# An LSTM and a three-layer FFN on one core: loads of the beginning asked for in another order, and the last half of the outputs cut in two

## The chip, the core and the metric

One Trainium2 chip; the kernel runs on one of its cores. The metric is device time in microseconds (us): the median of three runs. Besides, one execution was taken by the profiler; its rows are times from the start of its span.

The engines are named as in the profile: PE is the matrix engine, PEld its weight loads, DVE the vector engine, ACT the scalar engine, POOL the GpSimd engine, SP the engine that only issues transfers. SPq, ACTq and POOLq are the queues in which SP, ACT and POOL issue transfers (DMAs).

## The reference

Cut to what matters (x is 32 x 64 x 256 in float32, cond is 32 x 256; every k is a matrix of booleans):

```python
xW = einsum('ntd,dg->ntg', x, Wx) + b              # g: 4 gates of 256
for t in range(64):                                # LSTM, h starts as cond, c as 0
    a = xW[:, t] + h @ Wh
    i, f, o = sigmoid(a[:, :256]), sigmoid(a[:, 256:512]), sigmoid(a[:, 512:768])
    g = tanh(a[:, 768:])
    c = f * c + i * g
    h = o * tanh(c)
y = concatenate([hs, -hs], -1)                     # FFN, weights +1 or -1
y = relu(s0 * (y @ sign(k0))) * 2                  # 512 -> 1024
y = relu(s1 * (y @ sign(k1))) * 2                  # 1024 -> 1024
out = x + s2 * (y @ sign(k2))                      # 1024 -> 256
```

## The kernel before, in words

**Layout.** 128 partitions hold 4 quarters of the hidden width times 32 sequences. The LSTM's products (line 246 for x times Wx, line 305 for h times Wh) are float32 and use the PE as four blocks of 32 columns at once; the trace shows each of these matmuls as two records. The FFN's products are float32r: every activation is split into a rounded part (h) and a rest (l), and both are multiplied by the same weights, one after the other, with the weights loaded again for each.

**Order.** The order of the work is written out by hand (a manual schedule); each engine carries out its instructions in the order of the program, and waits at an instruction until its inputs are there. The loop over the 64 steps (line 702) runs on PE the matmuls of a step's gates, and between them fillers: first products of x with Wx for later steps, from step 21 on the FFN of blocks of 16 steps (512 columns: 16 steps times 32 sequences). The last block (lines 417 to 583) comes after the last step, when no step is left to be mixed with.

**The beginning** (lines 107 to 156 and 637 to 682). DVE writes zeros: a small tile `warm`, then `idle` of 128 x 512 bf16, then the two rows for the bias. SP and ACT issue loads: the first eight steps of x (line 133: four transfers of 64 KB, two on each queue), Wx for the first 128 of the 256 inputs (k = 0) and then for the others (k = 1): two gates at once on SP (256 KB), the other two one by one on ACT (128 KB each). Then follow the next eight steps of x, and Wh. POOL issues the load of `h_first` and then those of the bias rows and scales. On PE, two matmuls of zeros clear the banks of the gates (line 641) and eight more go to a bank that is not read (`p_idle`, line 643, `WARM_UP = 8`). After them come the products of x: for eight steps the two middle gates with k = 0, then the two outer gates with k = 0, then the bias (line 658), then all four gates with k = 1. These need x turned round by DVE (line 229, two instructions of four steps each, behind all four loads of x) and the part of Wx concerned.

**Transfers and semaphores.** Transfers of SP and ACT share eight semaphores in turn; a transfer whose semaphore is still in use waits at its place in its queue until the one eight places earlier has landed.

**The end** (lines 550 to 583). The last layer of the last block has 128 output rows for m = 0 and as many for m = 1. The first eight of the 16 steps (half 0) are computed for both m, turned (line 385), scaled and added to x (line 388) and stored (line 380: four transfers of 64 KB, two on SP and two on ACT). The last eight steps (half 1) are computed for m = 0 and then for m = 1, each by 16 matmuls of 256 columns (8 blocks of inputs, h and l); each m is turned and scaled by itself, and one store of four transfers follows.

```python
        for m in range(2):
            layer2(1, m, [*range(K2, FC0), *range(K2)], True, True)
            turn_out(os[1], po_half[1, m], m)
            scale_out(os[1][:, :, m, :], xq[b, 1][:, :, ts(m, 32)])
        store(b, 1, os[1].rearrange("p t m j -> p t (m j)"), [nc.sync, nc.scalar])
```

## Time and profile before

| | |
|---|---|
| time, median of 3 runs | 312.36 us (312.21 to 312.55) |
| the profiled execution, whole time | 312.31 us |
| the profiled execution, its span | 310.5 us |
| PE busy | 304.5 us, 98% of the span, 4138 instructions |
| PEld busy | 242.7 us, 78% |
| DVE, ACT, POOL busy | 178.1, 142.0, 6.6 us |
| first warm-up matmul begins | 1.24 us |
| first product of x begins | 5.44 us |
| gates of step 0 begin | 16.84 us in the chain of waits |
| last matmul begins | 305.66 us |
| last instruction of DVE begins | 306.46 us |

The whole time has about 1.8 us outside the span. A row of the timeline has its start, how long it lasts, engine, line, operation, output and inputs, and in brackets the idle time before it with what ended it. The ends of matmuls are modelled: the distance from one start to the next is the better measure of their rate. In the chain of waits, each piece has its start, its length, and the engine and tile that the end of the kernel hung on in that time.

### The profile page before, as it was taken

To read this page: it belongs to the slowest core of one execution; us is meant where nothing else is said; L and a number is where in the kernel's file an instruction comes from. 1 tells how busy PE (TensorE), PEld (TensorE's weight loads), DVE (VectorE), ACT (ScalarE), POOL (GpSimd) and SP (SyncE) were. 2 spreads that over 40 slices of the span, in tenths; PEclk is the share of its full clock that TensorE was granted. 3 is DMA by queue.
4 is the path that set the end of the run, shared out by engine and by line. 5 is a ranking of instruction groups with operands and counts; after the bars stand their busy time and mean duration, and the time that the engine had idled before them with its cause. 6 is when DMAs were issued, how large, how long until landed. Compare 5 with 4: busy or idle time off the path is not lost.

```text
span 310.5 us, 9798 instructions
## 1 busy us (share of the span) xinstructions
PE 304.5 (98%) x4138; PEld 242.7 (78%) x4138; DVE 178.1 (57%) x530; ACT 142.0 (46%) x512; POOL 6.6 (2%) x24
## 2 busy tenths in 40 slices
PE   8999999999999999999999999999999999999994
PEld 4888888788777777777777777777777777899993
DVE  2566767777673444355754445567554434698543
ACT  0225566774564543435633434355443333886220
POOL 5300000000000000000000000000000000000000
PEclk9999999999999999999999999999999999999999
DMA  6874001142000000000010000000310000131002
GB/s 192 206 196 99 5 19 38 36 95 65 3 2 0 2 2 0 3 2 0 2 38 22 14 3 0 2 2 13 92 34 2 3 0 2 31 79 27 2 0 69
DMA packets 30587, 10.89 MB, mean 35 GB/s; under 512 B 27720, under 2 KB 29768, under 8 KB 30544
## 3 DMA queue, kind: packets, MB, share of 16 engines
q1 hardware_dynamic: 27136, 8.66, 11.2%
q10 hardware_dynamic: 3168, 1.57, 2.0%
q8 instruction: 32, 0.52, 0.7%
q0 software_dynamic: 240, 0.04, 0.1%
q14 instruction: 11, 0.09, 0.1%
HBM read 8.16 MB, written 2.10 MB: 33 GB/s over the span
## 4 chain that ended last, share of the span: by engine, by line
PE 97%; DVE 1%; ACT 0%; issue 0%; ACTq 0%
PE p L617 30%; PE gates L305 20%; PE px L246 18%; PE p L591 8%; PE po L604 7%; PE gates L452 4%; PE po L561 2%; PE r L452 2%; PE x L452 2%; PE p L479 2%; PE p_idle L643 1%; PE gates L641 0%; DVE a_7l L362 0%; DVE o L388 0%; PE p_bias L658 0%
## 5 line engine op out<-in xcount | busy, mean ns | idle before, releaser
L305 PEld LDWEIGHTS gates<-wh,hist 128*32 128x32 f32 x2016 | 54.6, 109 | 22.3 <-issue 13.4
L305 PE MATMUL gates<-wh,hist 128*32 128x192 f32 x2016 | 68.1, 275 | 0.0
L246 PE MATMUL px<-wx,xT 128*32 128x256 f32 (+1 forms) x1168 | 60.5, 353 | 0.1
L322 ACT ACTIVATE sig<-gates 128x128 f32<-128x128 f32 x64 | 17.7, 277 | 80.6 <-PE gates L305 80.4
L246 PEld LDWEIGHTS px<-wx,xT 128*32 128x32 f32 x1168 | 42.4, 110 | 11.3 <-DVE c_first L652 0.7
L326 DVE TENSOR_TENSOR kept<-sig,c 128x64 f32<-128x64 f32 x63 | 14.2, 225 | 50.0 <-ACT sig L322 49.7
L332 ACT ACTIVATE th<-c 128x64 f32<-128x64 f32 x64 | 16.4, 257 | 31.4 <-DVE c L330 31.4
L334 DVE TENSOR_TENSOR h<-sig,th 128x64 f32<-128x64 f32 x64 | 14.4, 225 | 20.7 <-ACT th L332 20.7
L262 DVE TENSOR_TENSOR xg<-px,bias 128x512 f32<-128x512 f32 x32 | 21.2, 671 | 2.8 <-PE px L246 2.3
L316 ACT COPY gates<-xg 128x192 f32<-128x192 f32 x64 | 20.0, 313 | 1.3 <-DVE xg L262 1.3
L591 PE MATMUL p<-hhi,w 128*128 128x512 f32 x48 | 19.3, 402 | 0.0
L591 PE MATMUL p<-hlo,w 128*128 128x512 f32 x48 | 19.1, 398 | 0.0
L339 DVE STREAM_TRANSPOSE hist<-h 128x64 f32<-128x64 f32 x64 | 15.7, 245 | 2.4
L330 DVE TENSOR_TENSOR c<-kept,new 128x64 f32<-128x64 f32 x64 | 14.4, 224 | 2.2
L324 ACT ACTIVATE sig<-gates 128x64 f32<-128x64 f32 x64 | 14.9, 233 | 0.1
L323 ACT ACTIVATE cand<-gates 128x64 f32<-128x64 f32 x64 | 14.0, 218 | 0.0
L328 DVE TENSOR_TENSOR new<-sig,cand 128x64 f32<-128x64 f32 x64 | 13.9, 217 | 0.0
L317 ACT COPY gates<-xg 128x64 f32<-128x64 f32 x64 | 13.0, 203 | 0.0
L591 PEld LDWEIGHTS p<-hhi,w 128*128 128x128 f32 x48 | 9.0, 188 | 2.2
L591 PEld LDWEIGHTS p<-hlo,w 128*128 128x128 f32 x48 | 9.0, 188 | 2.0
L211 ACT ACTIVATE w<-bits,nsgn,sgn 128x1024 fp32r<-128x1024 uint8 x8 | 9.9, 1241 | 0.0
L617 PE MATMUL p<-a_7h,w 128*128 128x512 f32 x24 | 9.9, 413 | 0.0
(249 smaller groups left out, 602.8 us busy)
## 6 DMA issues: line engine op xcount, KB each, us to landing
x<-in_x_dram SPq DMA_DIRECT2D x60, 64.0 KB, 2.8
out_dram<-o SPq DMA_DIRECT2D x28, 64.0 KB, 1.8
bits<-in_L_ffn_k_dram SPq DMA_DIRECT2D x10, 128.0 KB, 3.2
wx<-in_L_cond_Wx_dram SPq DMA_DIRECT2D x2, 256.0 KB, 4.2
wx<-in_L_cond_Wx_dram ACTq DMA_DIRECT2D x4, 128.0 KB, 4.6
wh<-in_L_cond_Wh_dram ACTq DMA_DIRECT2D x2, 256.0 KB, 5.6
wh<-in_L_cond_Wh_dram SPq DMA_DIRECT2D x2, 256.0 KB, 6.2
k<-in_L_ffn_k_dram SPq DMA_DIRECT2D x2, 256.0 KB, 3.1
```

What stands on the lines that cost most here:

```text
L246: nc.tensor.matmul(p[q * N : (q + 1) * N, t % 2, slots], xT[i // 2, i % 2][:, s, k, :], wx_q[:, k, q, slots], start=start, stop=False, ski ...
L262: nc.vector.tensor_tensor(xg[t], p.rearrange("p t g j -> p t (g j)"), b, ALU.add)
L305: nc.tensor.matmul(g[q * N : (q + 1) * N], hT[:, k, :], wh_q[:, k, q, slots], start=False, stop=(k == 1), skip_group_check=True,)
L316: nc.scalar.copy(gates[0], x_t[:, :3])
L322: nc.scalar.activation(sig[:, 0:2, :], gates[0][:, 1:3], AF.Sigmoid)
L324: nc.scalar.activation(sig[:, 2, :], gates[1][:, 0], AF.Sigmoid)
L332: nc.scalar.activation(th, c, AF.Tanh)
L339: nc.vector.transpose(hT, h.rearrange("p (j b) -> p b j", b=2))
L452: nc.tensor.matmul(bank[pair][:, i], a(k)[:, ts(2 * pair + i, P)], b(k, n), start=first and i == 0 and k == 0 and n == 0, stop=last and k ...
L591: nc.tensor.matmul(p, w0[:, k, ts(m, P)], a[:, k, :], start=(n == 0), stop=(n == 3))
L604: nc.tensor.matmul(po[m], w2[:, m, k], a1[k][n], start=(k == 0 and n == 0), stop=(k == FC1 - 1 and n == 1))
L617: nc.tensor.matmul(p1[m], w1[:, k, ts(m, P)], a0[k][n], start=(k == 0 and n == 0), stop=(k == FC0 - 1 and n == 1),)
```

## The change

At the beginning:

- `idle` becomes 128 x 128 and is written first; the matmuls of zeros read it four times over, so that they keep their 512 columns. `WARM_UP` goes from 8 to 7.
- The first eight steps of x are asked for in two halves of four steps (eight transfers of 32 KB). Between the halves, the two middle gates of Wx with k = 0 are asked for as two transfers of 64 partitions, one on each queue. After the second half come the outer gates with k = 0, one on each queue, then with k = 1 three gates at once on SP (384 KB) and the fourth on ACT.
- POOL issues the bias rows ahead of `h_first`.

At the end: half 1 with m = 1 is computed as two lots of four steps, each by 16 matmuls of 128 columns into a bank of its own; each lot is turned, scaled and stored by itself, with both m, as four transfers of 32 KB.

```diff
-    WARM_UP = 8
+    WARM_UP = 7
...
+    idle = const.tile([P, P], mybir.dt.bfloat16, name="idle")
+    nc.vector.memset(idle, 0.0)
     nc.vector.memset(warm, 0.0)
-    idle = const.tile([P, 512], mybir.dt.bfloat16, name="idle")
-    nc.vector.memset(idle, 0.0)
...
-    load_x(0, 0, both)
-    for k in range(2):
-        load_gates(wx, wx_d, (1, 2), [nc.sync], slice(k, k + 1))
-        for slot in (0, 3):
-            load_gates(wx, wx_d, (slot,), [nc.scalar], slice(k, k + 1))
+    first_x = [slice(0, SB // 4), slice(SB // 4, SB // 2)]
+    load_x(0, 0, both, first_x[0])
+    load_gates(wx, wx_d, (1, 2), both, slice(0, 1))
+    load_x(0, 0, both, first_x[1])
+    load_gates(wx, wx_d, (3,), [nc.sync], slice(0, 1))
+    load_gates(wx, wx_d, (0,), [nc.scalar], slice(0, 1))
+    load_gates(wx, wx_d, (1, 2, 3), [nc.sync], slice(1, 2))
+    load_gates(wx, wx_d, (0,), [nc.scalar], slice(1, 2))
...
-        for m in range(2):
-            layer2(1, m, [*range(K2, FC0), *range(K2)], True, True)
-            turn_out(os[1], po_half[1, m], m)
-            scale_out(os[1][:, :, m, :], xq[b, 1][:, :, ts(m, 32)])
-        store(b, 1, os[1].rearrange("p t m j -> p t (m j)"), [nc.sync, nc.scalar])
+        o = os[1].rearrange("p t m j -> p t (m j)")
+        ks = [*range(K2, FC0), *range(K2)]
+        layer2(po[1][:, :CB], 0, 1, ks, True, True)
+        turn_out(os[1], po[1][:, :CB], 0)
+        scale_out(os[1][:, :, 0, :], xq[b, 1][:, :, :32])
+        for i in range(2):
+            steps, p = ts(i, SB // 4), last_po[i][:, : CB // 2]
+            layer2(p, 1, 1, ks, True, True, ts(i, CB // 2))
+            turn_out(os[1][:, steps], p, 1)
+            scale_out(os[1][:, steps, 1, :], xq[b, 1][:, steps, 32:])
+            store(b, 1, o, [nc.sync, nc.scalar], slice(i * SB // 4, (i + 1) * SB // 4))
...
+    zeros = idle.unsqueeze(1).to_broadcast([P, TB // P, P])
     for g in gate_banks:
-        nc.tensor.matmul(g, idle[:, :P], idle, start=True, stop=True)
+        nc.tensor.matmul(g, idle, zeros, start=True, stop=True)
     for n in range(WARM_UP):
-        nc.tensor.matmul(p_idle, idle[:, :P], idle, start=True, stop=True)
+        nc.tensor.matmul(p_idle, idle, zeros, start=True, stop=True)
```

`store` gains an argument for the steps that it stores, and `layer2` takes the bank, the half and the columns in place of a table of banks. The matmuls of half 0 stay as they are, as does everything between the beginning and the end.

More of the change, by code (lines that the diff above doesn't have):

```diff
@@ L143, in lstm_ffn @@
     nc.scalar.activation(warm[:, 1:2], warm[:, :1], AF.Sigmoid)
-    h_first = const.tile([P, HQ], F32, name="h_first")
-    nc.gpsimd.dma_start(out=h_first, in_=cond.rearrange("n (q j) -> q n j", q=NQ))
     b_rows = b_d.rearrange("(o g h) -> o g h", o=1, g=4)
@@ L149, in lstm_ffn @@
     nc.gpsimd.dma_start(out=b_row[1][:1], in_=b_rows[:, 1:3])
+    h_first = const.tile([P, HQ], F32, name="h_first")
+    nc.gpsimd.dma_start(out=h_first, in_=cond.rearrange("n (q j) -> q n j", q=NQ))
     scales = []
@@ L375, in output, with store @@
             yield
-    def store(b, half, o, engines):
+    def store(b, half, o, engines, part=slice(0, SB // 2)):
         t0 = b * SB + half * (SB // 2)
@@ L380, in store @@
             engines[q % len(engines)].dma_start(
-                out=out[:, t0 : t0 + SB // 2, ts(q, HQ)], in_=o[q * N : (q + 1) * N]
+                out=out[:, t0 + part.start : t0 + part.stop, ts(q, HQ)], in_=o[q * N : (q + 1) * N, part]
             )
@@ L550, in last_block, with layer2 @@
         po = [ps_o.tile([P, TB], F32, tag="po", name=f"po{b}_{m}") for m in range(2)]
-        po_half = {
-            (0, 0): po[0][:, :CB],
-            (0, 1): po[0][:, CB:],
-            (1, 0): po[1][:, :CB],
-            (1, 1): ps_f.tile([P, TB], F32, tag="pf", name=f"po{b}_2")[:, :CB],
-        }
-        def layer2(half, m, ks, first, last):
+        last_po = [ps_f.tile([P, TB], F32, tag="pf", name=f"po{b}_{2 + i}") for i in range(2)]
+        def layer2(p, m, half, ks, first, last, cols=slice(0, CB)):
             for k in ks:
@@ L561, in layer2 @@
                     nc.tensor.matmul(
-                        po_half[half, m],
+                        p,
                         w2[:, m, k],
-                        a1[k, half][n],
-                        start=first and k == ks[0] and n == 0 and (half, m) != (0, 1),
+                        a1[k, half][n][:, cols],
+                        start=first and k == ks[0] and n == 0,
                         stop=last and k == ks[-1] and n == 1,
@@ L572, in last_block @@
             for m in range(2):
-                layer2(0, m, ks, ks[0] == 0, ks[0] > 0)
+                layer2(po[0][:, ts(m, CB)], m, 0, ks, ks[0] == 0 and m == 0, ks[0] > 0)
         for m in range(2):
-            turn_out(os[0], po_half[0, m], m)
+            turn_out(os[0], po[0][:, ts(m, CB)], m)
         o = os[0].rearrange("p t m j -> p t (m j)")
@@ L639, in lstm_ffn @@
     p_idle = ps_f.tile([P, TB], F32, tag="pf", name="p_idle")
+    zeros = idle.unsqueeze(1).to_broadcast([P, TB // P, P])
     for g in gate_banks:
-        nc.tensor.matmul(g, idle[:, :P], idle, start=True, stop=True)
+        nc.tensor.matmul(g, idle, zeros, start=True, stop=True)
     for n in range(WARM_UP):
-        nc.tensor.matmul(p_idle, idle[:, :P], idle, start=True, stop=True)
-    turn_x(0, 0, slice(0, SB // 4))
-    turn_x(0, 0, slice(SB // 4, SB // 2))
+        nc.tensor.matmul(p_idle, idle, zeros, start=True, stop=True)
+    for part in first_x:
+        turn_x(0, 0, part)
     for i in range(4):
```

## The prediction

> **What bounds the kernel now.** I read the page first, engines and then the chain that ended last:

> ```profile
> PE 304.5 (98%) x4138; PEld 242.7 (78%) x4138; DVE 178.1 (57%) x530; ACT 142.0 (46%) x512; POOL 6.6 (2%) x24
> ...
> PE 97%; DVE 1%; ACT 0%; issue 0%; ACTq 0%
> ```

> PE is busy in 98% of the span, and 97% of the chain that ended last lies on it. Between the first product of x and the last matmul no other engine stands in the chain for more than a few us, so the middle, which the change leaves alone, moves as one block. What counts is when PE starts useful work, whether it stalls early, and what follows its last matmul. So next comes the chain of waits for the first 12 us (start, length, what):

> ```profile
> 0.91 0.28 DVE idle L110
> 1.19 0.05 issue
> 1.24 1.03 PE gates L641 x2
> 2.27 3.23 PE p_idle L643 x8
> 5.51 1.89 PE px L246 x64
> 7.39 0.12 issue
> 7.51 1.96 PE px L246 x64
> ```

> PE waits for the zeros until 1.24, multiplies zeros until about 5.4, begins the products of x, and halts at 7.39: the second 64 records need the outer gates of Wx, which ACT asked for last. The timeline of the end:

> ```profile
> 305.54 0.28 PE L561 MATMUL po<-c_1h,w 128*128 128x256 f32 x1
> 305.54 0.19 PEld L561 LDWEIGHTS po<-c_1l,w 128*128 128x128 f32 x1
> 305.66 0.28 PE L561 MATMUL po<-c_1l,w 128*128 128x256 f32 x1
> 305.98 0.45 DVE L385 STREAM_TRANSPOSE o<-po 128x256 f32<-128x256 f32 x1 [0.95 <-PE po L561]
> 306.46 0.48 DVE L388 SCALAR_TENSOR_TENSOR o<-o,total,x 128x256 f32<-128x256 f32 x1
> 306.97 0.81 SPq L380 DMA_DIRECT2D out_dram<-o  x2
> 306.98 0.88 ACTq L380 DMA_DIRECT2D out_dram<-o  x2
> ```

> Matmuls of 256 columns start every 0.12 us. From DVE's start to the end of the span (310.5) pass 4.5 us: 1.0 on DVE, then the store.

> **The beginning, step by step.** (a) The zeros: DVE's 40-element fill took 92 ns and the 256-element one 272, so 0.83 ns an element; 64 elements take about 112 ns. Written first, from 0.82, they are there at 0.93, and PE starts 0.05 later at 0.98 instead of 1.24. (b) Nine matmuls of zeros instead of ten. Their weight loads start 0.427 us apart (2.07, 2.50, 2.92), while 512 columns later take 0.227 (line 479: 32 in 7.25): half the rate. The trace's record of the full clock starts at 5.20. Nine end at 0.98 + 9 x 0.427 = 4.82; about 0.10 lay between the last of them and the first product; so products start at 4.90 instead of 5.44. If the clock still comes at 5.20, the first 0.30 us run at half rate and lose 0.15: the gain is 0.54 - 0.15 = 0.39. If the clock comes 0.26 earlier with the work it is 0.5; if it comes half a us later, 0.1. I take 0.39, with the clock where the row has it. (c) The stall: one set of 64 records takes 1.75 us where nothing is missing (7.51 to the bias at 9.26). The first set should then be done at 5.44 + 1.75 = 7.19, and the second began at 7.51: 0.33 lost.

> Does the data come in time? Before, the 256 KB of x were followed by the middle gates (issued 1.66, landed at 5.0, three stragglers of 16 after 4.3, beside the 4 KB packets of `h_first`), and the outer ones landed at 6.15 and 7.38. After, only 128 KB of x stand ahead of the middle gates, whose halves go on both queues at about 1.6. First data came 1.0 us after an issue; 384 KB at the 200 to 270 GB/s of the transfer view are through by about 3.5, landed by 4 to 4.3, ahead of 4.90. The second half of x is needed at about 5.9; its second transfers wait for a semaphore of the first (about 2.7) and should land by 4.5. The outer gates, asked for at about 3.1, should land by 5.3 to 6.0; they are needed at 4.90 + 0.15 + 1.75 = 6.8. So the 0.33 goes; the bounds are nothing and all of it. Beginning: 0.39 + 0.33 = **0.72 gained**, bounds 0 and 0.9.

> At no cost: `h_first` is asked for some 2 us later and is first read by DVE at 14.04; it landed at 5.3. Queues: SP has 11 transfers ahead of the next x instead of 8, ACT 11 instead of 10. Wh is behind them; it landed at 14.9 and is needed at 16.84 before, at 16.1 after: 1.2 us of cover, which three more issues of 0.33 to 0.47 could just use up, but Wh's own wait is for earlier landings (issued only at 7.2 to 8.1), which come sooner.

> **The end, step by step.** (d) 16 matmuls of 256 columns become 32 of 128, and each still loads 128 x 128 weights. No row shows a float32r matmul under 256 columns. Columns alone: 512 take 0.227 and 256 take 0.120, so 128 would take 0.067. But weights must be in the array first, and where PE comes back from the gates, the weight loads show their own pace:

> ```profile
> 98.02 0.19 PEld L617 LDWEIGHTS p<-a_4l,w 128*128 128x128 f32 x1
> 98.13 0.19 PEld L617 LDWEIGHTS p<-a_5h,w 128*128 128x128 f32 x1
> 98.36 0.19 PEld L617 LDWEIGHTS p<-a_5l,w 128*128 128x128 f32 x1
> ```

> The first two are 0.11 apart, since the second starts once the first's matmul does, and nothing ran in front of it; the third waits for a matmul of 512 columns. 43 such pairs in the trace stand 108 or 109 ns apart, one 107, none closer. The load of 32 columns lasts 109 ns and that of 128 lasts 188: 0.82 ns a column, 105 for 128. So I take 0.109 a matmul: weights, not columns, set the pace. 32 x 0.109 - 16 x 0.120 = 3.49 - 1.92 = **1.57 lost**. Bounds: 0.067, 0.21 lost; 0.227, if 128 columns went at float32's four passes (line 305 does 512 columns of a step, all four blocks, in 0.87 where one pass of 512 is 0.21), 5.33 lost.

> [...]

> (e) The last matmul is shorter: 0.39 for 512 columns and 0.28 for 256 make 0.05 less for 128. (f) DVE's last two: turning took 0.245 for 64 columns and 0.45 for 256, so 0.31 for 128; scaling took 0.75 for 512 and 0.48 for 256, so 0.35. With their gaps 0.73 in place of 1.00: 0.27 gained. The lots are at least 16 x 0.067 = 1.07 apart, so the first lot's 0.73 on DVE is out of the way. (g) The last store moves 128 KB instead of 256. Before, 2.5 us passed from the first issue (306.97) to the last landing; the 256 KB moved in 1.3 of them (307.75 to 309.05), one queue's transfer behind the other's. Each queue's second issue still comes 0.36 to 0.42 after its first, and a store takes 1.8 to 2.0 to land. Half the data would save 0.65; with the issues in front, 0.40. Bounds 0 and 0.65. The first lot's four transfers are issued over a us earlier and are through by then; the semaphores that the last four wait for are those of half 0, landed long before.

> End: 1.57 - 0.05 - 0.27 - 0.40 = **0.85 lost**.

> **Sum.** 0.85 - 0.72 = 0.13 lost, on 312.31: 312.44. The profiled run is 0.05 under the median of 312.36, so I say 312.4. With i for the pace of the small matmuls the whole is 32 i - 3.36 us: nothing at i = 0.105, 0.62 lost at 0.124, 0.62 gained at 0.086. A measurement of this kernel can tell 0.2%, or 0.62 us, from no change.

> **Rivals.** *Columns set the pace* (i = 0.067): 1.22 gained, 311.1. For it: at 256 columns the pace is still the columns' (0.120 is 0.107 less than 512's). Against it: 44 pairs, none under 107 ns. It decides below i = 0.086. *Four passes* (i = 0.227): 3.9 lost, 316.2. It ends on the slow side, in the 32 small matmuls, and decides from i = 0.124. For it: no float32r row under 256 columns; against: 512 and 256 columns go at one pass. *The beginning gives nothing*: the middle gates land after 4.9, or the stall moves to another load, or Wh comes late. Then the end's 0.85 stands alone, 313.2. For it: landings had stragglers of up to 0.8 us; against: half as much is asked for ahead.

> **Numbers.** My forecast 0.60, columns 0.18, four passes 0.08, nothing at the beginning 0.14. The forecast's own range, with i from 0.105 to 0.120, the store's and the beginning's bounds, is 311.9 to 313.2; it is same in 0.44, slower in 0.10, faster in 0.06. The empty beginning is slower in 0.09, same in 0.05. Together: faster 0.06 + 0.18 = 0.24; same 0.49; slower 0.10 + 0.08 + 0.09 = 0.27. The range of 311.0 to 313.4 takes in the columns' case and the empty beginning and leaves out the four passes.

> **What would show it.** The first warm-up at 0.98, products at 4.9, no gap between the two sets of 64. Weight loads of the last 32 matmuls 0.109 apart: 0.067 or 0.227 decides for a rival. DVE's last two at 0.31 and 0.35, and 2.1 from the last first issue to the last landing. I am wrong if the chain has PE waiting for Wx or Wh, or if the middle gets longer.

## The result, and the profile after

| | before | after |
|---|---|---|
| time, median of four runs | 312.43 us (312.21 to 312.55) | 315.53 us (315.30 to 315.83) |
| ratio, 95% interval | | 1.0097, 1.0082 to 1.0112 |
| profiled execution, its span | 312.31, 310.5 us | 315.30, 313.3 us |
| first product of x | 5.44 us | 5.07 us |
| gates of step 0 on PE, in the chain | 16.84 us | 18.45 us |
| first matmul of the last quarter (half 1, m = 1) | 303.86 us | 305.49 us |

The change costs 3 us, and the prediction (312.4, at most 313.4) was wrong. One run of those below, of `e4_h_first` at 319.77 us, lies far above the others of its kernel and is left out of times and ratios as a slow one.

The page after, engines and chain:

```profile
PE 306.0 (98%) x4153; PEld 242.0 (77%) x4153; DVE 178.7 (57%) x532; ACT 142.1 (45%) x512; POOL 6.6 (2%) x24
...
PE 94%; DMA 3%; DVE 1%; ACTq 0%; ACT 0%; issue 0%
```

DMA, which had no share in the chain before, has 3% of it (9.6 us), and PE is down from 97 to 94%. The chain of waits of the first 20 us (start, length, what) says which transfers:

```profile
1.67 3.30 DMA wx<-in_L_cond_Wx_dram
4.97 0.02 issue
5.00 6.29 DMA wx<-in_L_cond_Wx_dram
11.29 0.04 issue
11.33 7.12 PE px L249 x128
18.45 0.87 PE gates L308 x32
```

Both pieces are Wx. The second is a transfer that is asked for only when the first has landed; it is one of the second rows (k = 1). PE's timeline shows what that did (in brackets the idle time before, and what ended it):

```profile
0.99 1.03 PE L647 MATMUL gates<-idle 128*128 128x512 bf16 x2 [0.99 <-DVE warm L110]
1.81 3.10 PE L649 MATMUL p_idle<-idle 128*128 128x512 bf16 x7
5.07 1.08 PE L249 MATMUL px<-wx,xT 128*32 128x128 f32 x32
6.56 2.83 PE L249 MATMUL px<-wx,xT 128*32 128x128 f32 x96 [0.41 <-DVE xT L232]
9.20 0.66 PE L664 MATMUL p_bias<-b_row,warm 128*32 128x128 f32 x16
11.33 7.12 PE L249 MATMUL px<-wx,xT 128*32 128x256 f32 x128 [1.48 <-DMA wx<-in_L_cond_Wx_dram]
```

PE starts 0.25 earlier as forecast, and its first product comes 0.37 earlier. Then it halts twice: 0.41 us for the second half of x, and 1.48 us for the second rows of Wx. The gates of step 0 come 1.61 us late, and from there the middle runs as one block: the last quarter starts 1.63 us late. The span is 2.73 longer, so the end has lost the other 1.10. Its timeline:

```profile
308.90 0.28 PE L560 MATMUL po<-c_1l,w 128*128 128x128 f32 x1
309.21 0.32 DVE L388 STREAM_TRANSPOSE o<-po 128x128 f32<-128x128 f32 x1 [1.08 <-PE po L560]
309.56 0.35 DVE L391 SCALAR_TENSOR_TENSOR o<-o,total,x 128x128 f32<-128x128 f32 x1
```

The 32 small matmuls start at 305.49 to 308.90, 0.110 us apart; DVE's two take 0.32 and 0.35; the last store is asked for at 309.94 and landed at 312.18, 2.24 us (before: 306.97 to 309.45, 2.48).

### The profile page after: what moved, and what is told of

It is laid out like the page before. It is cut to its first block, busy times and chain, and to the rows that moved or that the text cites. A ratio compares the mean times of both kernels' runs of the same rounds, so it can differ in the third digit from the quotient of the medians.

```text
span 313.3 us, 9842 instructions
## 1 busy us (share of the span) xinstructions
PE 306.0 (98%) x4153; PEld 242.0 (77%) x4153; DVE 178.7 (57%) x532; ACT 142.1 (45%) x512; POOL 6.6 (2%) x24
## 4 chain that ended last, share of the span: by engine, by line
PE 94%; DMA 3%; DVE 1%; ACTq 0%; ACT 0%; issue 0%
PE p L622 30%; PE gates L308 20%; PE px L249 17%; PE p L596 8%; PE po L609 7%; PE gates L455 4%; DMA wx<-in_L_cond_Wx_dram 3%; PE po L560 3%; PE r L455 2%; PE x L455 2%; PE p L482 2%; ACTq L93 0%; DVE a_7l L365 0%; DVE o L391 0%; DVE o L388 0%
## 5 line engine op out<-in xcount | busy, mean ns | idle before, releaser
L249 PEld LDWEIGHTS px<-wx,xT 128*32 128x32 f32 x1168 | 40.1, 110 | 15.8 <-DMA wx<-in_L_cond_Wx_dram 1.7
L327 ACT ACTIVATE sig<-gates 128x64 f32<-128x64 f32 x64 | 14.9, 232 | 0.2
```

The source lines that it names most:

```text
L249: nc.tensor.matmul(p[q * N : (q + 1) * N, t % 2, slots], xT[i // 2, i % 2][:, s, k, :], wx_q[:, k, q, slots], start=start, stop=False, ski ...
L327: nc.scalar.activation(sig[:, 2, :], gates[1][:, 0], AF.Sigmoid)
```

## Experiments

Ratios are to the kernel before on the same chip (312.6 to 312.8 us in these runs), with 95% intervals.

### The two parts by themselves

`e1_head_only`: all edits of the beginning, and lines 550 to 583 and `store` as before.

> The new beginning with the old end. In the changed kernel's trace the last layer's second half for m = 1 begins at 305.49 us, 1.63 later than before (303.86). Theory 'the beginning lost it, by late transfers of Wx': this kernel takes about 1.6 us more than before (314.0), gates of step 0 begin near 18.4 and PE halts about 1.5 us ahead of the k = 1 products. Rival 'the end lost it, the late start is an accident of one execution': 311.7, the 0.72 gained that was forecast.

Measured: 314.83 us, 1.0065 (1.0042 to 1.0088): 2.0 us lost. The first theory holds; in this profile PE waits 1.86 us for the second rows.

`e2_tail_only`: the reverse, the new end on the old beginning.

> The old beginning with the new end. Theory 'beginning and end add up': about 1.1 us more than before (313.5), the small matmuls 0.111 us apart, as in the changed kernel's trace. Forecast of the prediction: 0.85 more (313.3). Rival 'the columns set the pace': no loss or a gain of 0.45.

Measured: 313.77 us, 1.0040 (1.0027 to 1.0054): 1.25 us lost. The two make 3.3, the change 3.0: they add up, within the intervals. Both parts lose.

### The end, piece by piece

`e9_two_lots_alone`: only the matmuls are halved.

```diff
-            layer2(1, m, [*range(K2, FC0), *range(K2)], True, True)
+            lots = 2 if m else 1
+            for i in range(lots):
+                layer2(1, m, [*range(K2, FC0), *range(K2)], True, True, ts(i, CB // lots))
```

> The kernel before, with its beginning, its stores and its DVE work on the last half as they were; only the 16 last matmuls of 256 columns become 32 of 128 (both lots in one bank, turned and scaled together as before). This is step (d) by itself. By the pace of 0.111 us seen in the profile after: 32 x 0.111 - 16 x 0.120 = 1.63 lost, and nothing given back: 1.0052 times the kernel before. By the prediction's 0.109: 1.57, 1.0050. If instead the columns set the pace (0.067): 0.22, 1.0007.

Measured: 314.55 us, 1.0062 (1.0048 to 1.0077), 1.9 us lost (1.5 to 2.4). In its profile the 32 last matmuls take 3.41 us from the first start to the last, where the 16 took 1.80, and DVE and the store take what they took before (1.31 us to the first issue, 2.48 to the last landing). That is 1.61 us by the profile, as forecast, and within the interval of the times.

`e10_four_lots_alone`: the same with four lots (`lots = 4 if m else 1`), 64 matmuls of 64 columns.

> As the two lots alone, with 64 matmuls of 64 columns. If the weight load of 128 columns sets the pace of a small matmul, whatever its columns, they stand 0.108 to 0.111 apart: 64 x 0.111 - 1.92 = 5.2 lost, 1.0166 times the kernel before. If a part of the 0.111 was still the 128 columns' own time, half the columns go faster: at 0.08, 3.2 lost, 1.010.

Measured: 320.85 us, 1.0261 (1.0244 to 1.0279), 8.2 us lost instead of 5.2. Up to 308.06 the matmuls start 0.112 apart, as expected; from then on 0.2135. The table by stretches (length, then PE, PEld, DVE, ACT, POOL busy and their counts, then the granted clock, DMA share, GB/s):

```profile
306.00:308.00 2.00, 2.00 (x20) 2.00 (x19) 0.00 (x0) 0.00 (x0) 0.00 (x0) 1.00 0.25 55
308.00:310.00 2.00, 2.00 (x12) 2.00 (x11) 0.00 (x0) 0.00 (x0) 0.00 (x0) 0.51 0.00 0
310.00:312.00 2.00, 2.00 (x11) 2.00 (x11) 0.00 (x0) 0.00 (x0) 0.00 (x0) 0.50 0.00 0
```

The granted clock fell to 0.50 although PE was never without work. While the clock was whole, 64 columns (0.112) went no faster than 128 (0.110 after), so the columns did not set the pace here. That the load of 128 x 128 weights set it agrees with the prediction's 43 pairs of weight loads, 0.108 to 0.109 apart.

`e11_dve_by_steps_alone`: the 16 matmuls undivided; turning, scaling and stores of the last quarter by four steps.

```diff
-            turn_out(os[1], po_half[1, m], m)
-            scale_out(os[1][:, :, m, :], xq[b, 1][:, :, ts(m, 32)])
-        store(b, 1, os[1].rearrange("p t m j -> p t (m j)"), [nc.sync, nc.scalar])
+            for i in range(m + 1):
+                steps = slice(i * SB // 2 // (m + 1), (i + 1) * SB // 2 // (m + 1))
+                turn_out(os[1][:, steps], po_half[1, m][:, ts(i, CB // (m + 1))], m)
+                scale_out(os[1][:, steps, m, :], xq[b, 1][:, steps, ts(m, 32)])
+                if m:
+                    store(b, 1, os[1].rearrange("p t m j -> p t (m j)"), [nc.sync, nc.scalar], steps)
```

> The kernel before, with its 16 last matmuls of 256 columns, and only the turning, the scaling and the stores of the last quarter of the outputs by four steps at a time. With the matmuls undivided both lots come to DVE at once: four operations (0.32, 0.35, 0.32, 0.35, with gaps some 1.40) in place of two (0.97), and the last store is asked for 0.43 later, of half the size, which the profile after showed to land 0.24 sooner. So 0.1 to 0.3 lost, 1.0003 to 1.001, if the first lot's stores are through in time; up to 0.7, 1.002, if eight stores one behind the other take as long as four whole ones. If steps (f) and (g) of the prediction held by themselves (0.27 and 0.40 to the good), it would gain 0.2 here.

Measured: 313.38 us, 1.0024 (1.0014 to 1.0035), 0.75 us lost, the upper case of the forecast. By the profile DVE is done at 307.32, but the last store is asked for at 307.63: each queue is still busy with its second issue of the first lot. It landed 2.30 after that, against 2.48 for a whole one. So half a store saved about 0.2 here, and its issue, queued behind another, came 0.3 late.

### The beginning: three suspects of which two fall

`e3_k1_split`: the beginning of e1, with the second rows in the pieces of before.

```diff
-    load_gates(wx, wx_d, (1, 2, 3), [nc.sync], slice(1, 2))
+    load_gates(wx, wx_d, (1, 2), [nc.sync], slice(1, 2))
     load_gates(wx, wx_d, (0,), [nc.scalar], slice(1, 2))
+    load_gates(wx, wx_d, (3,), [nc.scalar], slice(1, 2))
```

> The new beginning with the old end, but Wx with k = 1 asked for as before: two gates at once on SP (256 KB), one and one on ACT (128 KB each), in place of 384 KB on SP and 128 KB on ACT. Theory 'the one transfer of 384 KB is what is late' (issued 4.54, landed 11.02): the stall ahead of the k = 1 products shrinks from 1.5 us to under 0.5, and about 1 us of the loss goes (313.0). Rival 'transfers are slow in that stretch whatever their size, or issued too late because of the eight semaphores': no change within 0.3 us of the new beginning alone.

Measured: 315.04 us, 1.0079 (1.0063 to 1.0095). That the second rows come as 384 KB in one transfer is not the cause.

`e4_h_first`: the beginning of e1, with `h_first` ahead of the bias rows, where it was.

> The new beginning with the old end, but h_first asked for ahead of the bias rows, as before. Theory 'its 4 KB packets, now at 5.4 to 6.9 us, hold up the engines just when Wx with k = 1 starts to move': that transfer lands 1 us sooner or more and the kernel gains about 1 us on the new beginning alone, if the middle gates do not land later for it. Rival 'the packets only share the engines': within 0.3 us of the new beginning alone.

Measured: 314.72 us, 1.0075 (1.0054 to 1.0096). By the times its place is not the cause either. In its profile, which is of the fastest run (313.79), the loss only sits elsewhere: the big transfer of the second rows landed at 10.52 in place of e1's 11.54, but the middle gates at 5.08 and 5.67 in place of 4.55 and 5.00, and PE began at 5.76.

`e5_x_whole`: the beginning of e1, with x's first eight steps in four transfers ahead of the gates.

```diff
-    load_x(0, 0, both, first_x[0])
+    load_x(0, 0, both)
     load_gates(wx, wx_d, (1, 2), both, slice(0, 1))
-    load_x(0, 0, both, first_x[1])
```

> The new beginning alone (the old end), but the first eight steps of x asked for whole, in four transfers of 64 KB ahead of the gates, in place of eight of 32 KB with the middle gates between them. Theory A: eight DMA semaphores go round, each transfer takes one, and the eight small transfers of x hold them, so that the second rows of Wx are asked for only at 4.54 us, when the middle gates have landed. Without the split the ninth transfer waits for a piece of x (landed at about 3.0), is asked for at about 3.1, and should land by 8.5 to 9.5, ahead of PE's need at 9.9: PE's wait of 1.5 to 1.9 us goes, and the time falls from 314.8 to 312.4 to 313.2. Theory B: not when the rows are asked for but the slow moving between 6 and 10 us (some 150 GB/s) makes them late, and it comes from what moves at that time, the broadcasts of the three scales above all: the rows still land at about 11, and the time stays at 314.4 to 315.2.

Measured: 313.15 us, 1.0022 (1.0008 to 1.0037): 1.3 of the 2.0 us come back, and the intervals of e1 and e5 do not touch. When SP asked for the big transfer of the second rows, before, after and in e5 (start, length):

```profile
2.15 0.43 SPq L127 DMA_DIRECT2D wx<-in_L_cond_Wx_dram  x1
4.54 0.35 SPq L127 DMA_DIRECT2D wx<-in_L_cond_Wx_dram  x1
2.97 0.35 SPq L127 DMA_DIRECT2D wx<-in_L_cond_Wx_dram  x1
```

The list of transfers has, of after (count, KB each, median us from issue to landing; x's are its first eight steps):

```profile
wx<-in_L_cond_Wx_dram SPq DMA_DIRECT2D x1, 384.0 KB, 6.5
x<-in_x_dram ACTq DMA_DIRECT2D x4, 32.0 KB, 2.7
```

and of e5:

```profile
wx<-in_L_cond_Wx_dram SPq DMA_DIRECT2D x1, 384.0 KB, 5.6
x<-in_x_dram ACTq DMA_DIRECT2D x2, 64.0 KB, 2.6
```

The big transfer itself is 0.9 us faster in e5; the greater part, 1.57 us, is when it is asked for. After, twelve transfers stand ahead of it, so the thirteenth waits for the semaphore of the fifth, half of the middle gates, which landed at 4.53: issue at 4.54, landing at 11.02. In e5 eight stand ahead, so it waits for a piece of x: issue at 2.97, landing at 8.54, well before PE's need at 10.0. In the kernel before, the transfer of the second rows was one of the first eight, waited for none, and was asked for at 2.15. e5 changes a second thing, for the whole of x now stands ahead of the middle gates: their second half landed at 5.67, and PE began at 5.76. That it is the semaphore which holds the second rows back is read from the rows, where in both profiles the issue follows that landing by 0.01 us.

On the size of a transfer the rows show: 32 KB took 2.6 us to land on SP and 2.7 on ACT, 64 KB in e5 2.4 and 2.6, so half the size landed no sooner. No run here tries the halves of the partitions by themselves. The price that counted here was another, a semaphore for each piece: the second rows were asked for at 4.54 in place of 2.97.

### What moves beside the second rows

`e6_scales_late`: the beginning of e1, with the three broadcasts of the scales on SP's queue behind the next block's x.

```diff
-        nc.gpsimd.dma_start(out=s, in_=s_d.partition_broadcast(P))
...
+    for s, s_d in zip(scales, (s0_d, s1_d, s2_d)):
+        nc.sync.dma_start(out=s, in_=s_d.partition_broadcast(P))
```

> The new beginning alone (the old end), but the three broadcasts of the scales (128 pieces of 4 bytes each) are taken off GpSimd's queue and asked for on SP's behind the loads of the next x. Theory A (the semaphores hold the second rows of Wx back): issue at 4.5 and a landing at about 11 remain, and the time stays at 314.4 to 315.2. Theory B (the broadcasts, moving from 6.7 to 12.4, slow everything beside them): the rows, still asked for at 4.5, land at 8.5 to 9.5, the stretch from 6 to 10 us moves over 220 GB/s in place of some 150, PE's wait at about 10 goes, and the time falls to 312.8 to 313.4.

Measured: 313.43 us, 1.0027 (1.0017 to 1.0037): 1.2 us come back, and the intervals of e1 and e6 do not touch. The same two stretches of e1 and then of e6 (last column GB/s):

```profile
6.00:8.00 2.00, 2.00 (x62) 1.98 (x57) 0.53 (x2) 0.00 (x0) 0.00 (x0) 1.00 0.66 163
8.00:10.00 2.00, 2.00 (x80) 1.90 (x71) 0.00 (x0) 0.00 (x0) 0.16 (x1) 1.00 0.58 126
```

```profile
6.00:8.00 2.00, 1.89 (x68) 1.62 (x64) 0.53 (x2) 0.00 (x0) 0.00 (x0) 1.00 0.86 204
8.00:10.00 2.00, 2.00 (x74) 1.74 (x64) 0.00 (x0) 0.00 (x0) 0.00 (x0) 1.00 1.09 292
```

Without the broadcasts the engines move 204 and 292 GB/s there in place of 163 and 126, though the second rows are still asked for at 4.53; the big one landed at 10.24 in place of 11.54, not at the 8.5 to 9.5 expected, and PE still waited 0.47 us. Three transfers of 0.5 KB were dear to what moved beside them here. In the kernel before, their packets started between 6.4 and 8.4 us, and the second rows had landed by 8.1; after, they started between 6.3 and 11.0, beside second rows that landed at 11.3.

`e13_scales_first`: the beginning of e1, with the broadcasts at the head of POOL's queue.

> The new beginning alone (the old end), with the three broadcasts of the scales at the head of GpSimd's queue, ahead of the bias rows and h_first. Taken off that queue they gave back 1.2 us (313.43 with them late on SP's queue, 314.83 with them where the change has them). If it is the scales that slow whatever moves beside them, they now slow the middle gates and x, between 4 and 7 us, and no longer the second rows: these land at about 10.2 as with the scales late, and the time is 313.2 to 313.8 plus what PE's start loses (up to 0.5). If it is anything that GpSimd's queue moves between 6 and 12 us, the bias rows and h_first stand there now and do the same: the rows land at 11 or later and the time stays at 314.4 to 315.2.

Measured: 314.40 us, 1.0056 (1.0040 to 1.0072), on the border of the two forecasts (at most 314.3, at least 314.4); so were the landings of the second rows, 10.67 and 11.39. The stretch from 8 to 10 us recovered (262 GB/s), so it isn't the queue as such. But from 3 to 5 us, where the broadcasts now were, 134 and 138 GB/s moved in place of 237 and 242 in e1; the middle gates' second half landed at 6.01 in place of 5.00, and PE began at 6.10 instead of 5.09. The cost went where the broadcasts went. By what mechanism 0.5 KB slows the others is open.

`e14_both_undone`: both edits, of e5 and of e6.

> The new beginning alone (the old end) with both suspects taken away: x's first eight steps whole, and the scales late on SP's queue. If the two are all that the beginning lost, it gains what is left of the prediction's 0.72 over the kernel before, or nothing: 312.0 to 312.6 us, 0.998 to 1.000. If there is a third cause, 313 or more, as with x whole alone (313.15).

Measured: 313.25 us, 1.0023 (1.0008 to 1.0039), no better than e5: once the second rows are asked for early, no cost of the broadcasts shows. But the new beginning still loses 0.7 us. Its twelve runs fall into 312.5 to 313.7 and 314.4 to 314.9. The kernel before hardly has this scatter: 312.1 to 313.4 beside e5 and e14, and two of 23 runs, at 313.6 and 314.1, beside e12. The profile is of an upper run (314.77): one outer gate landed at 9.83 there, in e5's at 7.77.

### Is there a gain in the order at all?

`e7_zeros_only`: only the smaller zeros and nine products of them.

> The kernel before with only the smaller zeros, written first, and nine products of zeros instead of ten; loads and end as before. The prediction's steps (a) and (b) by themselves: products of x 0.54 us earlier and 0.39 gained would give 312.0. My theory now: the middle gates landed at 5.0 and the last outer ones at 7.38 in the kernel before, so products of x can start at 5.1 at the earliest and the second set of 64 cannot start before 7.5, whatever PE does before: the whole gain is swallowed by the stall at 7 us, which grows from 0.12 or 0.33 to 0.5 or 0.7, and the time is 312.3 to 312.5.

Measured: 312.42 us, 0.9993 (0.9985 to 1.0002): nothing, as the second theory had it. PE's timeline:

```profile
5.27 1.95 PE L246 MATMUL px<-wx,xT 128*32 128x128 f32 x64 [0.86 <-DMA wx<-in_L_cond_Wx_dram]
7.59 1.96 PE L246 MATMUL px<-wx,xT 128*32 128x128 f32 x64 [0.37 <-DMA wx<-in_L_cond_Wx_dram]
```

PE is ready earlier and waits for the middle gates, then again for the outer ones.

`e8_order_only` and, once more, `e17_order_only_again`: in addition the last outer gate of the first rows goes on SP, ahead of the second rows.

```diff
-        for slot in (0, 3):
-            load_gates(wx, wx_d, (slot,), [nc.scalar], slice(k, k + 1))
+        for slot, engine in ((0, nc.scalar), (3, both[k])):
+            load_gates(wx, wx_d, (slot,), [engine], slice(k, k + 1))
```

> As the one with the smaller zeros alone, and in addition one edit of the loads: the last outer gate of the first rows of Wx moves from ACT's fourth place to SP's, behind the middle gates and ahead of the middle gates of the second rows. All transfers stay whole. If the stall at 7 us is a matter of order, the outer gates land by 6.5, PE runs through from 5.1, the second rows (needed at about 9.0) still land by 8.5, and the time falls by 0.4 to 0.6 to 311.8 to 312.0. If the rate of the DMA engines sets the landings whatever the order (1 MB of Wx and 256 KB of x at some 250 GB/s, behind 2 us, is 7 to 8 us), the stall only moves from the outer gates to the second rows, and the time is 312.3 to 312.6.

> The kernel with the smaller zeros and the order of one gate changed, once more, beside the one with the middle gates first and against the kernel before on the same chip. It stood at 0.999 with an interval of 0.9978 to 1.0003; by its profile (gates of step 0 at 16.3 in place of 16.6) it should be 0.9990 again, and both intervals together tell whether it beats the kernel before.

Measured: 312.22 us, 0.9990 (0.9978 to 1.0003), and 312.53 us, 1.0011 (0.9993 to 1.0030). In the profiles the stall between the two sets is gone and the second rows are in time: matmuls of step 0's gates start at 16.27 and 16.17 against 16.60 before. So by the profiles the order has 0.3 to 0.4 us to give, but 4 of the 23 runs lie at 314.0 to 314.5, and no gain is shown. Whether a longer warm-up (e18) would keep it for this order was not tried.

`e12_order_and_queue`: e8 with `h_first` behind the bias rows and the scales late.

> The kernel before with its end; smaller zeros and nine products of them; all transfers whole, the last outer gate of the first rows of Wx moved from ACT's fourth place to SP's behind the middle gates; h_first behind the bias rows on GpSimd's queue; the three scales on SP's queue behind the loads of the next x. If h_first's 4 KB packets were what held the middle gates' last stragglers (landed 5.30, 13 of 16 engines at 4.56, with the order changed alone), they land by 4.7 and PE starts the products at 5.0 in place of 5.44; the outer gates land by 6.3, the second rows by 7.5, and the gates of step 0 come at about 15.9 in place of 16.6: 0.6 gained, 0.998 times the kernel before. If the stragglers come from elsewhere, it stands with the order alone: 0.3 gained, 0.999. If it costs that the scales stand on SP's queue (their 3 issues of 0.35 us ahead of the loads of the next weights), up to 0.3 is lost again.

Measured: 312.69 us, 1.0019 (1.0001 to 1.0038). The middle gates landed at 6.07, no sooner (5.30 and 5.20 in e8 and e17); `h_first` is not what holds them. Five of twelve runs at 314.0 to 314.6.

`e15_gates_first`: smaller zeros and whole transfers, the middle gates first on SP with the last outer gate and two gates of the second rows behind them, all of x on ACT ahead of the other gates.

```diff
-    load_x(0, 0, both)
+    load_gates(wx, wx_d, (1, 2), [nc.sync], slice(0, 1))
+    load_x(0, 0, [nc.scalar])
...
```

> The kernel before with its end; smaller zeros and nine products of them; all transfers whole, the middle gates first on SP's queue with the last outer ones and the second rows behind them, and the whole of x on ACT's queue ahead of the other gates. The middle gates are then asked for at 0.73 in place of 1.66, and x's last piece at 2.1 in place of 1.19. If both land by 4.5, PE starts the products at 4.9 when its zeros end, and runs through: 0.5 us sooner than with the order of one gate changed (gates of step 0 at 16.3 there), 311.6 to 312.0, 0.9975 to 0.9985 times the kernel before. If the 512 KB need until 5 us whatever the order, it starts at 5.3 and gains 0.2 to 0.3 over the kernel before, 0.999.

Measured: 319.47 us, 1.0217 (1.0204 to 1.0231), against 0.9975 to 0.999 expected. x's fourth piece got a semaphore in use and was asked for at 4.37; PE idled for 5.5 us, and then its clock was at half for 6.8 us:

```profile
6.00:8.00 2.00, 0.00 (x0) 0.00 (x0) 0.00 (x0) 0.00 (x0) 0.00 (x0) 0.77 0.70 191
8.00:10.00 2.00, 0.09 (x4) 0.09 (x8) 0.59 (x2) 0.00 (x0) 1.03 (x5) 0.50 1.10 281
10.00:12.00 2.00, 2.00 (x40) 1.85 (x44) 0.26 (x2) 0.00 (x0) 1.31 (x8) 0.50 0.94 221
```

`e16_gates_first_again`: x's fourth piece behind the middle gates on SP (`[nc.scalar, nc.scalar, nc.scalar, nc.sync]`).

> As the middle gates first (319.47, where x's fourth piece waited for a semaphore until 4.37), but x's fourth piece goes on SP's queue right behind the middle gates, so that the first eight transfers, one for each semaphore, are all that PE needs first. It is asked for at about 1.2 and lands by about 4.5, as do the middle gates; PE starts the products between 4.9 and 5.2, runs through the outer gates (asked for at 1.7 to 2.2, landed by 6), and the second rows land by 8 for a need at 9. No long idle, so the granted clock stays at 1.00. 0.3 to 0.6 gained over the kernel before: 0.998 to 0.999. If the four gates' order is worth nothing by itself and 512 KB land at 5.3 whatever the order, it stands with the order of one gate changed (0.999), or a little over it.

Measured: 315.15 us, 1.0067 (1.0043 to 1.0092), again no gain. x's third piece, asked for at 1.70 on ACT, landed at 6.80; PE idled for 3 us, and the clock was at half from 7.18 to 10.60. By this profile it is now x that comes last, and DVE turns it from 6.92 on (0.46 us) before PE's first product at 7.42.

### The scatter

`e18_longer_warm_up`: e12 with `WARM_UP = 9`, eleven products of zeros.

> As order and queue together, with eleven products of zeros in place of nine, so that PE works on zeros until 5.7 instead of 4.8. There the runs fell into two groups, seven of twelve at 312.2 to 312.7 and five at 314.0 to 314.6. Theory: the full clock is granted only at the end of a window of 3.41 us (all stretches of one clock in the records are multiples of it) in which PE worked some 78% or more, and the windows lie differently in each execution; after nine zeros PE idles 1.2 us until the gates land, and where a window holds that gap the clock comes one window later, which at half rate costs 1.7 us. With eleven, the gap is 0.5 at most and no window of the beginning can fail: the upper group goes, all runs are below 313.6, the median 312.3 to 312.8. Rival: the upper group are executions in which some gates land late; then eleven zeros change nothing, and some five of twelve stay above 313.9.

Measured: 312.60 us, all twelve runs at 312.23 to 313.48; 0.9998 (0.9988 to 1.0007). No run lies in the upper group, with the same loads, as the theory of the clock had it. The theory's share of some 78% is the author's estimate from the profiles before (77% in e3, 79% in e7 and e15). Two things are missing for a proof: e18 ran on another chip than e12, and no upper run of e12 was profiled. The kernel is no faster than before.

## Why the prediction was wrong, step by step

- **(a)** Right: PE began at 0.99 (0.98 forecast).
- **(b)** The last product of zeros starts 0.7 us earlier (4.37, before 5.05), but products began at 5.07, not 4.90: the middle gates landed at 4.53 and 4.97, not at 4 to 4.3. e7 shows that the earlier zeros by themselves gain nothing (0.39 forecast). The clock, for which the prediction took the row's 5.20, came at 4.69 after, before the first product; that was luck, for in e1 it came at 7.01.
- **(c)** The outer gates landed at 6.41 and 6.59 as needed (6.8 forecast as the need), and that stall went. The second half of x, "should land by 4.5", landed at 6.04 and made one of 0.41.
- **The step that failed** is the paragraph "Does the data come in time?". It follows the first rows and x, and ends there. The second rows of Wx are not in it, nor under "At no cost", where the lengths of the queues were counted against Wh alone. They were landed at 7.1 to 8.1 and needed at 9.70 before; the wait for a semaphore, which the paragraph applied to x, holds for them too, and moves their issue from 2.15 to 4.54. With the time from issue to landing grown from 5.0 (256 KB) to 6.5 (384 KB; 5.7 in e6, without the broadcasts beside it), that is the 11.02 and 11.29 of the profile. The rival "the beginning gives nothing" named a stall that moves to another load, and let it eat no more than the gain; it cost 2.0 beyond that (e1).
- **(d)** Right in kind and nearly in size: 1.57 forecast, 1.61 in the profile of e9; neither the columns (0.067) nor four passes (0.227) set the pace, for the small matmuls start 0.110 apart in after and e9.
- **(e)** Not there: from the last matmul's start to DVE's passed 0.31 us, against 0.32; 0.05 was forecast as gained.
- **(f)** Right: 0.32 and 0.35; 0.27 gained.
- **(g)** Too large: 0.24 (after) and 0.28 (e2) in place of 0.40. A last transfer of 32 KB landed 1.5 to 1.8 us after its issue (after), one of 64 KB at least 1.7 to 2.0 (before): half the size saved about 0.2.
- **The end** so lost 1.1 by the profile and 1.25 (0.84 to 1.69) by e2, against 0.85. **The beginning** lost 1.6 in the profile and 2.0 (1.3 to 2.7) by e1, against a gain of 0.72; this is nearly all of the error.

## What to carry to other kernels

When loads are put in another order, follow every one that an engine waits for within the stretch, to the last, through issue, semaphore and landing: here the first loads won 0.4 us and a later one, which nobody had looked at, lost 1.5. Count the transfers ahead against the semaphores that go round: here the pieces of x took the places of transfers that were free to start, and the second rows were asked for at 4.54 in place of 2.15. And a matmul cut from 256 to 128 columns with its weights unchanged cost nearly as much as the whole one here (0.110 against 0.120 us); there must be more behind it to hide than the 0.5 us here.

## What the runs showed of the hardware that was not expected

```profile
6.00:8.00 2.00, 1.98 (x40) 2.00 (x44) 0.00 (x0) 0.00 (x0) 0.00 (x0) 1.00 1.03 291
8.00:10.00 2.00, 1.78 (x36) 1.33 (x32) 0.00 (x0) 0.00 (x0) 0.00 (x0) 1.00 1.06 176
10.00:12.00 2.00, 2.00 (x76) 2.00 (x80) 0.00 (x0) 0.71 (x1) 0.00 (x0) 1.00 0.57 153
```

Another 3.41 us at half rate cost 1.7 us where PE has work throughout (half of 3.41: an estimate, from products of zeros that start 0.427 apart at first and matmuls of 512 columns that take 0.227 later), about the distance between the two groups of runs, and e18, which closes the gap, has no run in the upper one. The profile of e14 doesn't settle this: its second set needed the outer gate that landed at 9.83, so PE would have waited for it at full clock too. What bridged PE to loads that came late were products of zeros, of which the change saves one: with nine of them PE idled 1.20 us before its first product in e12, with eleven it ran through in e18.

**In e10 the clock fell with PE busy.** Behind 3.41 us full of matmuls of 64 columns, 0.112 apart, the granted clock went to 0.50, and it stayed there over the next two such stretches, as full, all with PE busy for 99% or more by the records. So the shares above are measured at the beginning only, and did not hold for these narrow matmuls. 32 of 128 columns did not bring the clock down (after, e2, e9), though they last only 3.4 us, so whether a longer row of them would is open.

**Open** besides is why single packets of the second rows took up to 1.6 us (at 6.0 us, after; up to 1.3 us in e6 too, so it isn't the broadcasts alone), against a median of 0.12 after 8 us.
